# Order of six VectorE instructions in a convolution's input transform, and a GpSimd addition in four pieces instead of two

## The chip, the cores and the metric

The kernel runs on one core of a Trainium2 chip. A core has five engines that work in parallel, each through its own queue in order: TensorE (PE, matrix products; PEld is its weight load), VectorE (DVE), ScalarE (ACT), GpSimd (POOL) and SyncE (SP, which here only issues transfers). They meet at semaphores. The metric is the device time of one execution in microseconds; lower is better.

## The reference

Input x is 32 x 128 x 2048 (batch, channel, length), all in float32. Two residual layers follow each other:

```
x = x + ffn0(cond0(x, c))      # cond0: a 128 x 128 channel mix per batch, a softmax-weighted sum of 8 matrices, plus a bias
                               # ffn0:  out = x W^T + bias, plus 16 low-rank updates scaled by coeffs * scales
x = x + ffn1(cond1(x, c))      # cond1: a grouped convolution over the length, 9 taps, padding 4, 4 groups, plus a context
                               # ffn1:  permuted columns, 16 heads: gelu(t up) down, columns put back
```

## The kernel before, in words

The length is cut into 4 phases of 512 columns (`NPH`, `QW`), and a phase into 4 runs of 128 (`NK`, `NM`). Batches are handled in 8 groups of 4 (`NG`, `GB`).

First, ffn0's weight is multiplied with x by a two-level fast matrix product of seven products each: seven rounds (`ROUNDS`), each over the 8 groups, each of these with seven products in `multiply` (L332). VectorE adds each product to the running sums (L325). Since the weight acts on the length and the mix of cond0 on the channels, this product is made first and the mix is applied to its result.

Then comes a pipeline over the 16 pairs of batches, c = 0 to 15. It begins in the last round, in the gaps that `multiply` leaves after each product (`between`), and goes on between the heads of ffn1 (`ffn_up`, L676, and `ffn_down`, L687). `stage(k, f)` calls a function for every pair with its own step number n = k - (8c - 21), from -2 to 9, so a new pair starts every 8 steps and two pairs overlap. For a pair:

- n = -2 and 1: `mix_loads` brings in one batch each (x, the parts of the product, the mix matrix).
- n = -1 and 2: `mix_bias` adds ffn0's bias `late["fb"]` to x on GpSimd (L427).
- n = 0 and 2: `mix_begin` and `mix_work`: ScalarE presets the banks (L435), TensorE mixes (L444), VectorE adds x (L447), SyncE spreads the result over `xg` (L451).
- n = 4 and 7: `conv_inputs(c, i, 0)` for half i = 0 and 1 of the channels: the six VectorE instructions L513 to L518, "a burst" below. They make from `xg` two difference pairs (each a 128 x 1024 result, an odd part o and an even part e side by side in `vb`) and from these v0 to v3 in `va`.
- n = 5 and 8: `conv_begin` (products of v0, then of v2, L534), and `conv_inputs(c, i, 1)`, which makes the two remaining inputs over `vb`.
- n = 6 and 9: `conv_middle` (products of v1, then of v3), `conv_end` (the two inputs in `vb`), `conv_rows`.

So n = 7 of a pair falls on the same step as n = -1 of the next: the burst of half 1 on VectorE and the bias addition on GpSimd are issued at the same step. In the last round GpSimd has also the sums of x for the next group, `x_combine` (L269 and L296 to L299). In the heads it also issues the indirect transfers of ffn1 (L660, L694).

The order of instructions is the order of the program: the schedule is written out by hand, no planner moves anything. A tile of the slot pool waits for the last readers of what its slot held before.

In the kernel before, both pairs are written to the same half of `vb[c]`, that of index i, one after the other; v1 is made before the second pair overwrites the first.

Of the kernel before, what the change touches and what calls it, by code (L numbers as in the profile page):

```python
# [11 lines left out]
ALU = mybir.AluOpType  # L12
# [12 lines left out]
NPH = 4  # L25
NK = 4
NM = QW // NK
# [24 lines left out]
def adaln_ffn_kernel(  # L52
# [16 lines left out]
    nc = tc.nc  # L69
# [8 lines left out]
    def slot(name, shape=(P, L)):  # L78
        return big.tile(list(shape), FP, name=name, tag="s")
# [314 lines left out]
    late, ins, pms, xgs, x1ts, va, vb, hts, open_ = {}, {}, {}, {}, {}, {}, {}, {}, {}  # L394
# [28 lines left out]

    def mix_bias(b):
        xt = ins[b][1]
        for f in (0, 2):
            nc.gpsimd.tensor_tensor(  # L427
                xt[:, f : f + 2], xt[:, f : f + 2], late["fb"][:, f : f + 2], ALU.add
            )

    def mix_begin(b):

# [63 lines left out]
    def conv_inputs(c, i, part):  # L496

        xg = xgs[c][i].rearrange("p r j n -> p (r j) n")
        d = [xg[:, :, k * NM : (k + 1) * NM] for k in range(NK)]
        tt, stt = nc.vector.tensor_tensor, nc.vector.scalar_tensor_tensor  # L500
        low, high = xg[:, :, 0 : 2 * NM], xg[:, :, 2 * NM : 4 * NM]
        if i == 0 and part == 0:
            vb[c] = slot(f"vb_{c}", (P, 2, 2, 4 * NM))
        if part == 0:
            va[c, i] = slot(f"va_{c}{i}", (P, 4, 4 * NM))
            v = [va[c, i][:, q].rearrange("p (r m) -> p r m", r=4) for q in range(4)]

            oe = vb[c][:, i].rearrange("p q (r m) -> p (q r m)", r=4).rearrange(
                "p (r k m) -> p r k m", r=4, k=2
            )  # L510
            o, e = oe[:, :, 0], oe[:, :, 1]
            both = oe.rearrange("p r k m -> p r (k m)")
            stt(both, low, -4.0, high, ALU.mult, ALU.add)  # L513
            tt(v[0], e, o, ALU.add)  # L514
            tt(v[1], e, o, ALU.subtract)  # L515
            tt(both, high, low, ALU.subtract)  # L516
            stt(v[2], o, 2.0, e, ALU.mult, ALU.add)  # L517
            stt(v[3], o, -2.0, e, ALU.mult, ALU.add)  # L518
        else:
            v0, v5 = (vb[c][:, i, q].rearrange("p (r m) -> p r m", r=4) for q in range(2))  # L520
            stt(v0, d[1], -5.0, d[3], ALU.mult, ALU.add)
            stt(v5, d[2], -1.25, d[0], ALU.mult, ALU.add)
            w0, w5 = v0[:, :, 1:NM], v5[:, :, 0 : NM - 1]
            stt(w0, d[3][:, :, 0 : NM - 1], 4.0, w0, ALU.mult, ALU.add)
            stt(w5, d[0][:, :, 1:NM], 0.25, w5, ALU.mult, ALU.add)
# [83 lines left out]
    def stage_first(c, n):  # L609
        if n in (-2, 1):  # L610
            mix_loads(2 * c + (n == 1))
        if n in (-1, 2):
            mix_bias(2 * c + (n == 2))
# [19 lines left out]
    def third_rest(c, n):  # L633
        if n in (6, 9):
            conv_rows(c, int(n == 9))
        if n == 3:
            residual_rows(c, 0, 0)
            residual_rows(c, 0, 1)
        if n in (4, 5, 7, 8):
            conv_inputs(c, int(n > 5), n in (5, 8))  # L640
        if n in (4, 5):
            residual_rows(c, 1, n - 4)
        if n == 8:
            xgs.pop(c)
# [326 lines left out]
    for k, (g, h) in enumerate(heads):  # L971
# [5 lines left out]
        t = ts.pop(k)  # L977
# [75 lines left out]
```

## Time and profile before

| | us |
|---|---|
| median of 3 runs (lowest to highest) | 2651.13 (2650.91 to 2654.36) |
| the profiled execution, its own time | 2649.93 |
| its span, from the first to the last instruction | 2648.2 |
| bias on GpSimd, L427, 64 instructions of 128 x 1024 | 155.5, mean 2448 ns |
| difference pairs on VectorE, L513 and L516, 32 each | 55.4 and 42.0, mean 1733 and 1313 ns |
| v0, v1 (L514, L515), 32 each | 35.3 and 25.1, mean 1103 and 784 ns |
| v2, v3 (L517, L518), 32 each | 25.0 and 26.2, mean 780 and 818 ns |

The mean granted clock of TensorE was 0.997 of full. In the profile, a line of a view names the engine, the line of the kernel, the operation, what it writes and reads (`va<-vb`), its shape and, in brackets, how long the engine had been idle before and what ended that. A float32 matmul of 128 x 512 runs as two instructions.

### The profile page before, as it was taken

How to read it: one execution, taken by the hardware profiler on the slowest of the kernel's cores; microseconds unless marked ns; L12 is line 12 of the kernel's file. 1: busy time of each engine (PE TensorE's matmuls, PEld its weight loads, DVE VectorE, ACT ScalarE, POOL GpSimd, SP SyncE). 2: the span in 40 equal slices, each digit the busy share in tenths (PEclk: the TensorE clock that was granted, in tenths of full speed). 3: DMA queues.
4: the chain of work that ended last, by engine and by line, in shares of the span. 5: the costliest groups of instructions: out<-in, count | busy, mean ns of one | idle time of the engine just before them, and what ended most of it. 6: DMA issues, size and time to landing. Idle time of an engine off the chain costs nothing.

```text
span 2648.2 us, 20100 instructions
## 1 busy us (share of the span) xinstructions
PE 2620.2 (99%) x6484; PEld 1234.3 (47%) x6484; DVE 1335.3 (50%) x2168; ACT 535.2 (20%) x1103; POOL 1200.2 (45%) x950
## 2 busy tenths in 40 slices
PE   9999999999999999999999999999999999999998
PEld 4444444444444444444444445555455544555543
DVE  5554134343233454433366666666666666666610
ACT  0000000000000000000011144444444444444432
POOL 7321536978756644756332333333433333333222
PEclk9999999999999999999999999999999999999999
DMA  8542458688466577565657788777678777777532
GB/s 317 201 163 103 163 194 325 266 327 351 153 247 254 221 284 288 222 256 201 226 203 240 221 304 283 234 220 232 228 248 255 224 227 227 239 240 237 164 126 88
DMA packets 183609, 609.18 MB, mean 230 GB/s; under 512 B 16848, under 2 KB 88016, under 8 KB 139088
## 3 DMA queue, kind: packets, MB, share of 16 engines
q1 hardware_dynamic: 150080, 474.79, 50.8%
q0 software_dynamic: 32992, 132.14, 14.5%
q8 instruction: 52, 0.85, 0.1%
q10 hardware_dynamic: 432, 0.96, 0.1%
q14 instruction: 53, 0.43, 0.0%
HBM read 372.42 MB, written 201.85 MB: 217 GB/s over the span
## 4 chain that ended last, share of the span: by engine, by line
PE 95%; DVE 2%; DMA 1%; issue 1%; SPq 0%; ACT 0%; POOLq 0%; DVEq 0%; ACTq 0%
PE bank L332 49%; PE bank L676 16%; PE bank L687 16%; PE bank L534 6%; PE bank L444 4%; PE bank L210 2%; PE bank L172 1%; DMA xg<-x 1%; DVE va L514 0%; DVE vb L513 0%; DVE vb L516 0%; DMA ws<-in_ffw 0%; DVE va L515 0%; DVE va L517 0%; DMA bf_sb<-in_BfT 0%
## 5 line engine op out<-in xcount | busy, mean ns | idle before, releaser
L676 PE MATMUL bank<-t,ws 128*128 128x512 f32 x1024 | 460.7, 593 | 1.0 <-DVE u L325 0.5
L687 PE MATMUL bank<-gl,ws 128*128 128x512 f32 x1024 | 460.2, 592 | 0.0
L694 POOL DMA_INDIRECT out<-t,orow x128 | 151.7, 1185 | 562.3 <-DVE t L692 493.8
L325 DVE TENSOR_TENSOR u<-bank,u 128x512 f32<-128x512 f32 x280 | 187.6, 688 | 418.0 <-PE bank L332 411.0
L679 ACT ACTIVATE gl<-bank 128x512 f32<-128x512 f32 x512 | 306.0, 598 | 447.3 <-PE bank L676 445.1
L332 PE MATMUL bank<-P_t,s_P 128*128 128x512 f32 x896 | 393.7, 592 | 0.0
L687 PEld LDWEIGHTS bank<-gl,ws 128*128 128x128 f32 x1024 | 194.8, 190 | 232.7 <-issue 230.8
L676 PEld LDWEIGHTS bank<-t,ws 128*128 128x128 f32 x1024 | 194.6, 190 | 228.0 <-issue 219.2
L332 PE MATMUL bank<-wo_P,s_P 128*128 128x512 f32 x640 | 283.1, 595 | 1.5 <-DVE u L325 1.5
L332 PE MATMUL bank<-wo_P,xt 128*128 128x512 f32 x640 | 281.5, 592 | 0.0
L332 PEld LDWEIGHTS bank<-P_t,s_P 128*128 128x128 f32 x896 | 170.5, 190 | 213.2 <-issue 211.2
L435 ACT ACTIVATE bank<-w,aggb 128x512 f32<-128x512 f32 x128 | 80.8, 684 | 890.2 <-DVE ags L406 872.6
L427 POOL TENSOR_TENSOR x<-x,fb 128x1024 f32<-128x1024 f32 x64 | 155.5, 2448 | 226.1 <-DMA x<-in_x 176.1
L692 DVE TENSOR_TENSOR t<-bank,t 128x512 f32<-128x512 f32 x128 | 87.9, 687 | 318.0 <-PE bank L687 318.0
L269 POOL TENSOR_TENSOR xt<-xt,xt 128x512 f32<-128x512 f32 x128 | 159.6, 1280 | 157.7 <-DMA xt<-in_xT 157.7
L332 PE MATMUL bank<-P_t,xt 128*128 128x512 f32 x448 | 201.5, 593 | 0.0
L325 DVE TENSOR_TENSOR p<-bank,p 128x512 f32<-128x512 f32 x112 | 77.5, 692 | 238.8 <-PE bank L332 238.8
L296 POOL TENSOR_TENSOR s_P<-xt 128x512 f32<-128x512 f32 x56 | 71.8, 1283 | 272.1 <-DMA xt<-in_xT 215.8
L332 PEld LDWEIGHTS bank<-wo_P,s_P 128*128 128x128 f32 x640 | 122.3, 191 | 154.2 <-issue 152.5
L332 PEld LDWEIGHTS bank<-wo_P,xt 128*128 128x128 f32 x640 | 121.7, 190 | 152.1 <-issue 150.1
L406 DVE SCALAR_TENSOR_TENSOR ags<-mix,att_bc,ags 128x128 f32<-128x128 f32 x224 | 155.9, 696 | 4.5
L660 POOL DMA_INDIRECT t<-hx_d,row x128 | 124.8, 975 | 59.9 <-issue 24.7
(144 smaller groups left out, 2649.6 us busy)
## 6 DMA issues: line engine op xcount, KB each, us to landing
xt<-in_xT SPq DMA_DIRECT2D x88, 1024.0 KB, 8.9
u<-u_d SPq DMA_DIRECT2D x40, 1024.0 KB, 11.3
wo_P<-wb_d SPq DMA_DIRECT2D x36, 1024.0 KB, 14.2
u<-c_d SPq DMA_DIRECT2D x64, 512.0 KB, 5.9
x<-in_x SPq DMA_DIRECT2D x32, 1024.0 KB, 8.0
xg<-x SPq DMA_DIRECT2D x256, 128.0 KB, 5.6
hx_d<-x1t SPq DMA_DIRECT2D x32, 1024.0 KB, 5.3
hx_d<-ht SPq DMA_DIRECT2D x32, 1024.0 KB, 7.0
```

The source lines that it names most:

```text
L269: nc.gpsimd.tensor_tensor(out[:, i, j], a[:, i, j], b[:, i, j], op)
L325: nc.vector.tensor_tensor(to, ps, to, ALU.add)
L332: nc.tensor.matmul(ps, lhsT=lhs[k][:, bass.ts(kc, P)], rhs=rhs[k][kc], start=first and kc == 0, stop=last and kc == 3, skip_group_check=True,)
L406: nc.vector.scalar_tensor_tensor(ag, mix[:, k], att, ag, ALU.mult, ALU.add)
L427: nc.gpsimd.tensor_tensor(xt[:, f : f + 2], xt[:, f : f + 2], late["fb"][:, f : f + 2], ALU.add)
L444: nc.tensor.matmul(pm, lhsT=ag, rhs=u[:, f], start=False, stop=True, skip_group_check=True)
L534: nc.tensor.matmul(out, lhsT=w[:, 2 * i + r], rhs=rhs, start=first and r == 0, stop=last and r == 1, skip_group_check=True,)
L660: nc.gpsimd.indirect_dma_start(out=t.rearrange("p k t -> p (k t)"), out_offset=None, in_=hx_d[g].rearrange("l k t -> l (k t)"), in_offset= ...
L676: nc.tensor.matmul(pu, lhsT=w[:, m * P : (m + 1) * P], rhs=t[:, 0], start=True, stop=True)
L679: nc.scalar.activation(gl[m], pu, AF.Gelu)
L687: nc.tensor.matmul(pd, lhsT=w[:, (MC + m) * P : (MC + m + 1) * P], rhs=gl[m], start=(m == 0), stop=(m == MC - 1),)
L694: nc.gpsimd.indirect_dma_start(out=out, out_offset=bass.IndirectOffsetOnAxis(ap=orow[:, g, h : h + 1], axis=0), in_=t[:, 1], in_offset=None,)
```

## The change

The six instructions of a burst are put in another order. The first pair is written to the other half of `vb[c]`, 1 - i, and the second to half i, so that both are there at the same time; v1 is made after v2. The bias is added in four instructions of 128 x 512 in place of two of 128 x 1024. Sizes, tiles, and everything on TensorE, ScalarE and SyncE stay the same. In the changed kernel v0, pair 2, v2, v1 and v3 stand in lines L514 to L518 in this order; the bias is again L427.

```diff
     def mix_bias(b):
         xt = ins[b][1]
-        for f in (0, 2):
-            nc.gpsimd.tensor_tensor(
-                xt[:, f : f + 2], xt[:, f : f + 2], late["fb"][:, f : f + 2], ALU.add
-            )
+        for f in range(NPH):
+            nc.gpsimd.tensor_tensor(xt[:, f], xt[:, f], late["fb"][:, f], ALU.add)
...
-            oe = vb[c][:, i].rearrange("p q (r m) -> p (q r m)", r=4).rearrange(
-                "p (r k m) -> p r k m", r=4, k=2
-            )
-            o, e = oe[:, :, 0], oe[:, :, 1]
-            both = oe.rearrange("p r k m -> p r (k m)")
-            stt(both, low, -4.0, high, ALU.mult, ALU.add)
-            tt(v[0], e, o, ALU.add)
-            tt(v[1], e, o, ALU.subtract)
-            tt(both, high, low, ALU.subtract)
-            stt(v[2], o, 2.0, e, ALU.mult, ALU.add)
-            stt(v[3], o, -2.0, e, ALU.mult, ALU.add)
+            oes = [
+                vb[c][:, h].rearrange("p q (r m) -> p (q r m)", r=4).rearrange(
+                    "p (r k m) -> p r (k m)", r=4, k=2
+                )
+                for h in (1 - i, i)
+            ]
+            (o0, e0), (o1, e1) = ((t[:, :, 0:NM], t[:, :, NM : 2 * NM]) for t in oes)
+            stt(oes[0], low, -4.0, high, ALU.mult, ALU.add)
+            tt(v[0], e0, o0, ALU.add)
+            tt(oes[1], high, low, ALU.subtract)
+            stt(v[2], o1, 2.0, e1, ALU.mult, ALU.add)
+            tt(v[1], e0, o0, ALU.subtract)
+            stt(v[3], o1, -2.0, e1, ALU.mult, ALU.add)
```

## The prediction

> **What bounds the kernel now.** I read the page first, for the share of each engine and the chain that ended last, then the waits of TensorE alone, then the timeline around the longest of them. The profiled execution has a span of 2648.2 us.
>
> ```profile
> PE 2620.2 (99%) x6484; PEld 1234.3 (47%) x6484; DVE 1335.3 (50%) x2168; ACT 535.2 (20%) x1103; POOL 1200.2 (45%) x950
> ...
> PE 95%; DVE 2%; DMA 1%; issue 1%; SPq 0%; ACT 0%; POOLq 0%; DVEq 0%; ACTq 0%
> ```
>
> TensorE is busy for 99% of the span, and the change leaves its instructions and their order as they are. So only what TensorE waits for can be won. The waits of TensorE:
>
> ```profile
> PE bank L534 <- DVE va L517: 7.8, 6, 3.8
> PE bank L210 <- DVE w L213: 4.7, 3, 4.0
> PE bank L332 <- DVE u L325: 1.5, 1, 1.5
> ...
> PE bank L534 <- ACT cq L545: 1.3, 1, 1.3
> ...
> PE bank L676 <- DVE u L325: 0.5, 1, 0.5
> PE bank L676 <- DMA ws<-in_ffw: 0.4, 1, 0.4
> ```
>
> Columns: total us, times, longest. The L210 wait lies in the first 50 us, outside the change. The rest, 7.8 + 1.5 + 1.3 + 0.5 + 0.4 = 11.5 us, lies where convolution and mixing run. Its main part is the second product of conv_begin (L534) waiting for v2 (L517). By the timeline the six waits for L517 end at 1384.58 (3.80 us), 1441.17 (1.41), 1474.29 (0.46), 1525.27 (0.90), 1769.83 (0.56) and 2421.72 (0.67); the one put down to cq ends at 1915.68 (1.29), 0.15 us after that burst's v2 (1914.84 + 0.69), so it is a seventh. The longest, as the timeline has it (start, length, engine, line):
>
> ```profile
> 1372.71 5.63 POOL L427 TENSOR_TENSOR x<-x,fb 128x1024 f32<-128x1024 f32 x2 [27.51 <-DMA x<-in_x]
> ...
> 1373.70 2.44 DVE L513 SCALAR_TENSOR_TENSOR vb<-xg 128x1024 f32<-128x1024 f32 x1
> 1376.18 2.72 DVE L514 TENSOR_TENSOR va<-vb 128x512 f32<-128x512 f32 x1
> 1378.31 1.72 POOL L296 TENSOR_TENSOR s_P<-xt 128x512 f32<-128x512 f32 x1
> 1378.82 1.75 DVE L515 TENSOR_TENSOR va<-vb 128x512 f32<-128x512 f32 x1
> 1379.76 1.03 PE L534 MATMUL bank<-va,tw_l 128*128 128x256 f32 x4
> ...
> 1380.60 2.17 DVE L516 TENSOR_TENSOR vb<-xg 128x1024 f32<-128x1024 f32 x1
> ...
> 1382.81 1.63 DVE L517 SCALAR_TENSOR_TENSOR va<-vb 128x512 f32<-128x512 f32 x1
> ...
> 1384.58 1.35 PE L534 MATMUL bank<-va,tw_l 128*128 128x256 f32 x4 [3.80 <-DVE va L517]
> 1385.73 4.65 PE L444 MATMUL bank<-u,agl 128*128 128x512 f32 x7
> ```
>
> Two things are to be seen. First, VectorE and GpSimd take turns: L514 takes 2.72 us here and 0.69 in a burst with no GpSimd work beside it (the burst at 1520.7), and each DVE instruction ends about when the POOL one before it has ended plus its own time. The burst reaches v2 after 10.7 us; undisturbed ones take 4.5. Second, the wait costs more than its 3.80 us: the chain of waits gives the eight L444 matmuls after it 4.87 us and eight others 3.43, and the four L534 take 1.35 where after a short wait they take 1.10. That is 1.44 + 0.25 = 1.69 us of TensorE at reduced pace.
>
> **The skill.** "SBUF — State Buffer", section "Who interferes with whom": a DVE instruction with two SBUF inputs and a GpSimd one that reads SBUF exclude each other for a whole instruction. The trace agrees: L513 to L518 stretch, while L325 with its PSUM operand takes 0.69 beside a running L427. "TensorE: Matmul & The Clock Gate", "What's actually happening": after about 3.4 us idle the array runs at half rate. The trace agrees after 3.80 us, and shows the same after two waits of 1.41 and 1.47 close together (eight L332 from 1443.77 take 5.14 us for 3.43), which the section doesn't lead one to expect.
>
> **The change, part by part.**
>
> *Order of the six DVE instructions.* Now: difference pair 1, v0, v1, pair 2, v2, v3. Then: pair 1, v0, pair 2, v2, v1, v3. The same six, so v0 and the end of the six stay where they are; v2 comes one instruction earlier: 0.69 us undisturbed, 1.67 with a turn of GpSimd in between (L515's end, 1380.57, less L514's, 1378.90). v1 and v3 are read by conv_middle at the next step, v3 being the later in both orders, so v1's delay costs nothing; v3 is no later, and covers it. For half 1, pair 1 is written over what conv_end of half 0 reads; the VectorE instructions of that conv_end (L586, L589) already stand ahead in the same queue and need those products, so nothing new is waited for. This covers all 32 bursts.
>
> *The bias in four pieces.* 32 inputs x 4 = 128 POOL instructions for 64. A lone 128x512 takes 1.28 us (L269, L296) against 2.35 for a 128x1024 (L427's median): 4 x 1.28 - 2 x 2.35 = 0.4 us more per input, 13 us in all on an engine at 45%, hidden by its idle time. If that cover were gone it would be 13 us, but GpSimd's products, s_P, are read four products of 1.72 us or more later. What counts is the turn-taking: a burst that begins beside L427 now loses to two pieces of 2.35; afterwards each of four DVE instructions lets one short piece past. The price of a piece in turn is the unknown. Below, from this trace: L515 ends 1.67 after L514 and L517 1.67 after L516 (1382.77 to 1384.44), L516 2.20 after L515, each with one 512 piece (L296 to L298) in between; less 0.65 or 1.22 that is about 1.0 us. Above: the whole 1.28. I take 1.0, since it was measured at just such turns; the other end is the first rival. A gain of more than that is excluded by the alternation.
>
> *The seven waits afterwards.* First: piece one from 1372.71 to 1373.99, pair 1 to 1375.21, piece and v0 to 1376.88, piece and pair 2 (2.20) to 1379.08, piece and v2 to 1380.75; plus 0.14 to TensorE 1380.89. TensorE was ready at 1384.58 - 3.80 = 1380.78. So 3.7 of 3.80 go, and the reduced pace with them: 5.4 us.
> At 1474.29: v2 is a turn (1.67) earlier, wait gone, 0.46 + 0.23 for restarting the array (1.10 against 0.87 for four) = 0.7.
> At 1441.17: v2 is 1.3 earlier and the wait goes, but the next product, at 1443.77, waits 1.47 us for an L325 queued on VectorE behind the whole six and the transposes after them (the GpSimd work beside them is x_combine's, unchanged). It now waits 2.8: nothing won.
> At 1525.27: the same in small, L325 takes it back at 1527.78: nothing.
> The other three are of one kind:
>
> ```profile
> 1760.90 5.65 POOL L427 TENSOR_TENSOR x<-x,fb 128x1024 f32<-128x1024 f32 x2 [3.22 <-issue]
> ...
> 1764.37 2.73 DVE L514 TENSOR_TENSOR va<-vb 128x512 f32<-128x512 f32 x1
> ...
> 1769.83 1.10 PE L534 MATMUL bank<-va,tw_l 128*128 128x256 f32 x4 [0.56 <-DVE va L517]
> ```
>
> By the same steps from L513's start (1762.18, a piece just over): 1.22 + 1.67 + 2.20 + 1.67 gives v2 at 1768.94 instead of 1769.69, 0.75 earlier. That is more than 0.56, and than 0.67 at 2421.72; with 0.23 each for the restart 0.8 and 0.9. At 1915.68, 0.8 of 1.29.
> Sum: 5.4 + 0.7 + 0 + 0 + 0.8 + 0.9 + 0.8 = 8.6 us. Span 2648.2 - 8.6 = 2639.6; that execution's own time, 2649.93, becomes 2641.3. The median of the runs is 1.2 above it: 2651.13 - 8.6 = 2642.5.
>
> **The rivals.**
> *The turns cost the full 1.28.* Then v2 of the first burst comes at 1373.99 + 1.22 + 1.97 + 2.50 + 1.97 = 1381.65, the wait is 1.0, and 2.8 + 1.7 = 4.5 us are won; 0.7 at 1474; at 1762 v2 would be at 1769.84, no gain. Together 5.2: 2645.9. For: one lone piece is 1.28. Against: the measured turns.
> *Won, then given back.* TensorE is 5.4 us ahead from 1385 on and meets transfers that don't move with it. For: L427 waits 176.1 us for x in all, so transfers come close to the work. Against: the loads stand on SP's queue behind a store that waits for L325 (505.4 us over 36 times), which moves with TensorE. Only the later 0.7 + 2.5 stays: 2648.
> *Slower.* From 1690 on eleven bursts run beside L427; v2 then has 0.1 to 0.8 us to spare before TensorE asks for it in eight of them, nothing in three. If each of four turns costs 0.45 more than taken, v2 comes 1.0 later than before instead of 0.8 earlier: 1.0 less the spare of each, about 8 us over the eleven, and no gain at 1384: some 2659. It decides from about 0.75 late. Against: the turns in the trace would have to grow by 45%.
> That the change doesn't do what it says is no case: the instruction streams of the two kernels show v2 as fourth of six and four pieces per input.
>
> **How the numbers follow.** Forecast 0.58, full price 0.20, given back 0.12, slower 0.10. A measurement of this kernel can tell some 0.2%, 5.3 us, from no change. Full price lies on that line and is halved: faster 0.68, same 0.22, slower 0.10. The forecast's own range is 2639 to 2646: below, the wait at 1441 falling away as well, if x_combine's pieces come after the burst (2.9 us of waits and 1.7 of reduced pace at most); above, the input landing 0.5 us later. The range for 8 in 10 is 2637 to 2652, which takes in the first two rivals and leaves the slower one out.
>
> **What would show it.** TensorE's wait for v2 (then L516) of at most some 2 us in all, none over 1.1; the L444 after the first burst at 3.43 us for eight; L514 never above 2.0; the wait for L325 near 1443 grown to 2.8; GpSimd busy some 13 us more. The prediction is wrong if v2 still comes 10 us after the first burst's start, if waits for x or s_P appear on TensorE, or if head bursts reach v2 later than 8 us after their start.

## The result, and the profile after

The changed kernel takes 2638.9 us (median; 2637.23 to 2640.06) against 2651.02 for the kernel before: a ratio of 0.9953, 95% interval 0.9944 to 0.9963, so 9.8 to 14.8 us faster where 8.6 was forecast. The profiled execution has a span of 2635.5 us, 12.7 less. The page of the kernel after, engines' shares and the chain that ended last:

```profile
PE 2614.5 (99%) x6484; PEld 1230.3 (47%) x6484; DVE 1336.4 (51%) x2168; ACT 535.3 (20%) x1103; POOL 1230.7 (47%) x1014
...
PE 96%; DVE 2%; DMA 1%; issue 0%; SPq 0%; POOLq 0%; ACT 0%; DVEq 0%; ACTq 0%
```

TensorE is the bound as before, with the same 6484 instructions. GpSimd is busy 30.5 us longer. TensorE's waits in the kernel after (total us, times, longest):

```profile
PE bank L332 <- DVE u L325: 3.1, 1, 3.1
...
PE bank L534 <- DVE va L516: 0.7, 2, 0.5
PE bank L676 <- DMA ws<-in_ffw: 0.4, 1, 0.4
```

The wait for v2, now L516, is 0.7 us where it was 7.8 and the 1.3 put down to cq. The wait for L325 has grown from 1.5 to 3.1. The first burst in the timeline after:

```profile
1371.65 7.36 POOL L427 TENSOR_TENSOR x<-x,fb 128x512 f32<-128x512 f32 x4 [28.86 <-DMA x<-in_x]
1372.11 1.89 DVE L513 SCALAR_TENSOR_TENSOR vb<-xg 128x1024 f32<-128x1024 f32 x1
1374.03 1.64 DVE L514 TENSOR_TENSOR va<-vb 128x512 f32<-128x512 f32 x1
1375.60 2.28 DVE L515 TENSOR_TENSOR vb<-xg 128x1024 f32<-128x1024 f32 x1
1377.91 1.64 DVE L516 SCALAR_TENSOR_TENSOR va<-vb 128x512 f32<-128x512 f32 x1
1378.17 1.03 PE L534 MATMUL bank<-va,tw_l 128*128 128x256 f32 x4
...
1379.70 1.10 PE L534 MATMUL bank<-va,tw_l 128*128 128x256 f32 x4 [0.50 <-DVE va L516]
1380.64 3.60 PE L442 MATMUL bank<-u,agl 128*128 128x512 f32 x8
```

v2 is the fourth of the six and comes 7.4 us after the start instead of 10.7. Each VectorE instruction takes its turn after one short piece: 1.64 for 512 columns, 2.28 for 1024. The matmuls that follow the wait run at full pace (eight in 3.60 us by the timeline, whose last end overlaps the next; before, seven took 4.65). The burst in the heads that answers to the one at 1762 us:

```profile
1751.08 7.36 POOL L427 TENSOR_TENSOR x<-x,fb 128x512 f32<-128x512 f32 x4 [3.73 <-DMA x<-in_x]
...
1757.34 1.64 DVE L516 SCALAR_TENSOR_TENSOR va<-vb 128x512 f32<-128x512 f32 x1
...
1759.13 1.10 PE L534 MATMUL bank<-va,tw_l 128*128 128x256 f32 x4 [0.19 <-DVE va L516]
```

To compare kernels I use one number from each trace: the time that TensorE lost from 1300 us on, which is the distance between the starts of two neighbouring matmuls less the usual 0.43 us (0.21 for 256 columns), summed where it is above 0.04. It holds a wait, the restart after it and a stretch at reduced pace, in which a matmul takes longer than usual. Place by place, before and after:

| place (time before) | before | after | forecast gain | gain |
|---|---|---|---|---|
| first burst, 1384 | 5.7 | 0.7 | 5.4 | 5.0 |
| 1441 and 1444 | 4.8 | 3.4 | 0 | 1.5 |
| 1474 | 0.7 | 0 | 0.7 | 0.7 |
| 1525 and 1528 | 2.0 | 0.4 | 0 | 1.6 |
| heads, from 1600 | 3.3 | 0.9 | 2.5 | 2.4 |
| all, with the ws wait of 0.7 in both | 17.3 | 6.1 | 8.6 | 11.2 |

The other 1.5 us of the span were gone before 1300: the pipeline's very first burst, for half 0 of the first pair and with no bias beside it, begins at 1342.9 instead of 1344.4, before the change can act. It is a difference between two executions: in other profiles that burst begins between 1343.2 and 1347.4.

One profile is one execution, and two later ones show how far such places shift. The kernel before once more (e10) lost 17.9 us from 1300 us on, 6.3 of them at 1441 and 1444 and only 1.3 in the heads; the changed kernel once more (e7) lost 8.4 us, 5.1 of them at the place of 1441 and 1444, 1.1 at that of 1525 and 1528, and 0.7 in the heads.

### The profile page after: what moved, and what is told of

The parts are those of the page before. It is cut to its first block, busy times and chain, and to the rows that moved or that the text cites. A ratio compares the mean times of both kernels' runs of the same rounds, so it can differ in the third digit from the quotient of the medians.

```text
span 2635.5 us, 20243 instructions
## 1 busy us (share of the span) xinstructions
PE 2614.5 (99%) x6484; PEld 1230.3 (47%) x6484; DVE 1336.4 (51%) x2168; ACT 535.3 (20%) x1103; POOL 1230.7 (47%) x1014
## 3 DMA queue, kind: packets, MB, share of 16 engines
q0 software_dynamic: 32992, 132.14, 14.8%
## 4 chain that ended last, share of the span: by engine, by line
PE 96%; DVE 2%; DMA 1%; issue 0%; SPq 0%; POOLq 0%; ACT 0%; DVEq 0%; ACTq 0%
PE bank L332 50%; PE bank L676 16%; PE bank L687 16%; PE bank L534 6%; PE bank L442 4%; PE bank L210 2%; PE bank L172 1%; DMA xg<-x 1%; DMA ws<-in_ffw 0%; DVE vb L515 0%; DMA a_sb<-in_A 0%; DVE vb L513 0%; DVE va L514 0%; PE bank L801 0%; DVE va L516 0%
## 5 line engine op out<-in xcount | busy, mean ns | idle before, releaser
L325 DVE TENSOR_TENSOR u<-bank,u 128x512 f32<-128x512 f32 x280 | 187.6, 688 | 415.4 <-PE bank L332 405.7
L427 POOL TENSOR_TENSOR x<-x,fb 128x512 f32<-128x512 f32 x128 | 178.9, 1427 | 223.9 <-DMA x<-in_x 223.9
L325 DVE TENSOR_TENSOR p<-bank,p 128x512 f32<-128x512 f32 x112 | 77.5, 692 | 235.3 <-PE bank L332 232.1
L660 POOL DMA_INDIRECT t<-hx_d,row x128 | 132.3, 1034 | 57.2 <-issue 26.0
```

What stands on the lines that cost most here:

```text
L325: nc.vector.tensor_tensor(to, ps, to, ALU.add)
L427: nc.gpsimd.tensor_tensor(xt[:, f], xt[:, f], late["fb"][:, f], ALU.add)
L660: nc.gpsimd.indirect_dma_start(out=t.rearrange("p k t -> p (k t)"), out_offset=None, in_=hx_d[g].rearrange("l k t -> l (k t)"), in_offset= ...
```

## The experiments

### One part at a time

The theory is turn-taking at the port that VectorE and GpSimd share: the order saves v2 one instruction and its turn, the cut makes each turn shorter. Rivals: one of the two does it all.

Only the order (e1), the bias left in two pieces (the diff is against the kernel after):

```diff
-        for f in range(NPH):
-            nc.gpsimd.tensor_tensor(xt[:, f], xt[:, f], late["fb"][:, f], ALU.add)
+        for f in (0, 2):
+            nc.gpsimd.tensor_tensor(
+                xt[:, f : f + 2], xt[:, f : f + 2], late["fb"][:, f : f + 2], ALU.add
+            )
```

> Only the new order of the six instructions; the bias stays in two pieces of 1024 columns. Theory (both parts count, through turns at the shared port): in the first burst v2 follows pair 1, v0 and pair 2 behind two long pieces and one of x_combine: about 9.0 us after the burst's start instead of 10.7, the wait there about 2.1 us instead of 3.8, with or without the reduced pace after it (1.7); the wait of 0.46 near 1474 gone; in the heads v2 comes 0.6 earlier, so waits of 0.56, 0.67 and 1.29 become 0, 0.1 and 0.7. Together 5 to 9 us faster than before, some 2642 to 2646, and slower than the full change by 3 to 7. Rival, the order alone does it: 2639, wait at the first burst under 0.6. Rival, the pieces alone do it: within 2 us of before, waits as before.

Measured: 2645.34 us, 0.9981 of before (0.9974 to 0.9988). TensorE's waits in e1 (L536 is conv_begin's product there, L518 v2):

```profile
PE bank L536 <- DVE va L518: 3.4, 5, 1.9
PE bank L332 <- DVE u L325: 3.3, 1, 3.3
PE bank L149 <- DVE warm L146: 1.5, 1, 1.5
PE bank L678 <- DVE u L325: 1.1, 1, 1.1
```

v2 of the first burst comes after 8.9 us and the wait there is 1.94, as worked out (9.0 and 2.1). The wait near 1474 is gone.

Only the cut (e2), in the kernel before:

```diff
-        for f in (0, 2):
-            nc.gpsimd.tensor_tensor(
-                xt[:, f : f + 2], xt[:, f : f + 2], late["fb"][:, f : f + 2], ALU.add
-            )
+        for f in range(NPH):
+            nc.gpsimd.tensor_tensor(xt[:, f], xt[:, f], late["fb"][:, f], ALU.add)
```

> Only the bias in four pieces of 512 columns; the old order (v2 fifth of six). Theory: in the first burst v2 comes behind five VectorE instructions and as many turns: about 8.7 us after its start, the wait about 1.8 us instead of 3.8, with or without the reduced pace (1.7); the wait near 1474 stays at about 0.5 (no bias beside that burst); in the heads v2 comes no more than 0.1 earlier than before, so waits of about 0.5 stay. Together 2 to 7 us faster than before, 2644 to 2649. Rival, the pieces alone do it: 2639 with all waits gone. Rival, the order alone does it: within 2 us of before.

Measured: 2644.45 us, 0.9979 of before (0.9969 to 0.9988). TensorE's waits in e2 (L532 and L515 are conv_begin's product and v2):

```profile
PE bank L532 <- DVE va L515: 4.4, 4, 2.2
...
PE bank L332 <- DVE u L325: 1.5, 1, 1.5
```

v2 of the first burst comes after 9.2 us (8.7 worked out), the wait is 2.22; the waits of 1.41, 1.47 and 0.47 stay as they were. In the heads the expectation missed: one wait of 0.29 is left, not several of 0.5. Over the eleven bursts that run beside the bias there, v2 comes 6.8 us after the start on average before, 6.4 in e2, 6.2 in e1 and 6.0 after. But in e10, the kernel before once more, it is 6.4 as well, so these averages do not show what either part is worth in the heads.

So neither part alone does it. 5.2 us (e1) and 6.0 (e2) make 11.2 together; the full change has 12.1 in its own comparison and 11.3 in e7's.

### No bias at all

e3 is the kernel before with the call of the bias addition left out, so that its output lacks ffn0's bias:

```diff
     def stage_first(c, n):
         if n in (-2, 1):
             mix_loads(2 * c + (n == 1))
-        if n in (-1, 2):
-            mix_bias(2 * c + (n == 2))
```

> The kernel before, old order, with ffn0's bias left out altogether: GpSimd makes no addition to x, so x reaches the residual without that bias. Theory: the waits in the heads are all due to turns with the bias, so every burst there takes its undisturbed 4.5 us to v2 and none waits; the first burst still takes turns with x_combine and reaches v2 after about 7.5 us, wait about 0.6 us; bursts near 1432 and 1466 as before. Some 8 to 10 us faster than before, about 2642. Rival, the length of the burst itself sets the waits (not GpSimd): waits in the heads of 0.5 us and more remain.

Measured: 2637.06 us, 0.9951 of before (0.9936 to 0.9967). All TensorE waits of e3 from 1300 us on:

```profile
PE bank L332 <- DVE u L325: 1.3, 1, 1.3
...
PE bank L534 <- DVE va L517: 0.5, 1, 0.5
...
PE bank L674 <- DMA ws<-in_ffw: 0.2, 1, 0.2
```

With the old order and no bias, every burst of the heads takes 4.5 us to v2 and nothing waits there. GpSimd's addition is what stretches them, not the burst's own length. The gain, 13.4 us, is above the 8 to 10 expected, and the expectation missed two places. The first burst was undisturbed too (4.5, not 7.5): with no bias ahead of it in the queue, x_combine was done at 1370.9, before the burst began at 1372.4. And in the next burst v2 came after 5.5 us, not after 8.4 as before, so that of the two waits and the reduced pace near 1440, 4.8 us before, a wait of 1.25 and its restart were left.

### How finely the bias is cut

The new order, with one addition of 2048 columns per input (e5) and with eight of 256 (e6):

```diff
-        for f in range(NPH):
-            nc.gpsimd.tensor_tensor(xt[:, f], xt[:, f], late["fb"][:, f], ALU.add)
+        nc.gpsimd.tensor_tensor(xt, xt, late["fb"], ALU.add)                    # e5
...
+        for f in range(NPH):                                                    # e6
+            for h in (slice(0, NQ), slice(NQ, QW)):
+                nc.gpsimd.tensor_tensor(xt[:, f, h], xt[:, f, h], late["fb"][:, f, h], ALU.add)
```

> The new order, the bias in one instruction of 128 x 2048 for each input (about 4.5 us from the 1.08 us that each further 512 columns cost). Theory of turns: in the first burst pair 1 waits for the whole piece, then v0, pair 2 and v2 take turns with x_combine: v2 about 10.4 us after the start, wait about 3.5 us; in the heads one long turn only, so v2 comes between 5 and 8.5 us after the start, by how late in the piece the burst begins. Some 4 to 6 us slower than the full change, 2643 to 2645. Rival, only the sum of GpSimd's work beside a burst counts, not its cut: v2 at about 7.5 us and 2639.

> The new order, the bias in eight instructions of 128 x 256 (about 0.7 us each, from the same slope). Theory of turns: each of the four VectorE instructions lets one short piece past, about 0.45 us in turn; v2 of the first burst about 5.5 to 6 us after its start, no wait there; heads at most 6 us. About 1 us faster than the full change, since only 0.5 + 0.2 + 0.1 us of waits for v2 and their restarts are left there: 2637 to 2638.5. Rival, the sum of GpSimd's work counts, or a short piece has a fixed cost near that of a long one: v2 at 7.4 us or later, time 2639 or more.

The first burst in the timeline of e6 (L514 to L517 are pair 1, v0, pair 2, v2):

```profile
1373.29 9.28 POOL L428 TENSOR_TENSOR x<-x,fb 128x256 f32<-128x256 f32 x8 [28.54 <-DMA x<-in_x]
1373.68 1.42 DVE L514 SCALAR_TENSOR_TENSOR vb<-xg 128x1024 f32<-128x1024 f32 x1
1375.13 1.10 DVE L515 TENSOR_TENSOR va<-vb 128x512 f32<-128x512 f32 x1
...
1376.15 1.74 DVE L516 TENSOR_TENSOR vb<-xg 128x1024 f32<-128x1024 f32 x1
1377.93 1.10 DVE L517 SCALAR_TENSOR_TENSOR va<-vb 128x512 f32<-128x512 f32 x1
...
1379.74 1.89 PE L535 MATMUL bank<-va,tw_l 128*128 128x256 f32 x8
```

v2 comes after 5.35 us, and conv_begin's eight matmuls run through without a wait. A turn costs 1.10 - 0.69 = 0.4 us here, against 1.64 - 0.69 = 0.95 with 512 columns. In the eleven head bursts v2 comes after 5.2 to 5.7 us, 4.9 to 7.1 after the change, 4.5 to 8.0 in e5: the finer the cut, the narrower the spread, because it matters less where in a piece the burst begins. GpSimd's bias takes 216.0 us in e6 and 145.4 in e5, so it is not the sum of its work that counts. The time of e6 is 2639.11, above the 2637 to 2638.5 expected and 0.7 less than the full change beside it (2639.77): within their spread. So the shorter turns are shown by the trace, a shorter time than the full change's is not.

e5 takes 2652.06 us, 0.9997 of before (0.9989 to 1.0006), and so is worse than expected. Its first burst:

```profile
1376.15 4.51 POOL L426 TENSOR_TENSOR x<-x,fb 128x2048 f32<-128x2048 f32 x1 [25.53 <-DMA x<-in_x]
1378.83 2.92 DVE L512 SCALAR_TENSOR_TENSOR vb<-xg 128x1024 f32<-128x1024 f32 x1
...
1387.44 1.10 PE L533 MATMUL bank<-va,tw_l 128*128 128x256 f32 x4 [1.52 <-DVE va L515]
```

The burst began 2.7 us into the piece, so v2 took 8.5 us and not 10.4. What the expectation missed lies elsewhere: a wait of 1.98 at 1355 for L325 with a reduced pace behind it, three waits of 0.7 to 0.8 in the heads, and one of 0.9 at 1582 of ffn_down's product for the mix's addition (L444 there, L447 before). With one piece the bias costs all that the new order brings.

### What is left: L325 behind the burst

After the change the longest wait is 3.14 us at 1437.19. The forecast took it to be one for an addition queued behind the whole burst and its transposes. In e4, during the last round, v1, v3 and the transposes of the residual are issued one product later, behind that addition:

```diff
-            tt(v[1], e0, o0, ALU.subtract)
-            stt(v[3], o1, -2.0, e1, ALU.mult, ALU.add)
+            def rest():
+                tt(v[1], e0, o0, ALU.subtract)
+                stt(v[3], o1, -2.0, e1, ALU.mult, ALU.add)
+
+            put_off(rest)
...
-            residual_rows(c, 1, n - 4)
+            put_off(lambda: residual_rows(c, 1, n - 4))
...
         def between(j):
+            catch_up()
```

`put_off` keeps a function for the next `catch_up` in the last round, and calls it at once in the heads.

> The full change, and in the last round v1, v3 and the transposes of the residual are issued one product later, behind VectorE's next addition. Theory: what is left of TensorE's waits, 3.1 us at 1437, is for an addition (L325) queued behind the whole burst and its transposes; with v1, v3 and four transposes out of its way (about 2.7 us and one turn of 1.0 or two) the wait falls to 0 to 1 us. Some 1.5 to 3 us faster than the full change, 2636 to 2637.5. Rival, that wait is set by TensorE's own order or by a transfer: it stays at 3 us and the time at 2639. Rival, the put-off work delays the addition after it by as much: a new wait for L325 one product later, time within 1 us of the full change.

> The full change as it is, beside the next three on one chip. Theory: 2639 (2637 to 2641), v2 of the first burst 7.4 us after its start, TensorE's wait there about 0.5 us, one wait of some 3 us for L325 near 1437 in the last round, with or without a stretch at reduced pace after it; the wait at the burst near 1510 to 1525 depends on when the last xg transfer lands. Rival, the extra 1.5 us won near 1525 belong to the change and not to that transfer: the wait there is again under 0.3 us whatever the transfer takes.

> The same kernel as e4, beside the full change on one chip. Theory: 3 to 4 us faster than the full change, 2635 to 2636, with no wait of TensorE for L325 in the last round. Rival, the difference between e4 and the full change was one of chips: within 1.5 us of it.

e4 takes 2635.11 us, 0.9937 of before (0.9924 to 0.9951). e7 is the full change and e8 is e4 once more, side by side: 2639.77 us (2637.37 to 2642.19) and 2635.51 (2632.35 to 2636.20), 0.9952 (0.9938 to 0.9965) and 0.9935 (0.9922 to 0.9949) of before. The spreads don't overlap; it is 4.3 us. No wait for L325 is left from 1300 us on in e4 and e8, and no new one came. Lost time there is 1.9 and 2.1 us, 8.4 in e7. The 4.3 us are more than the wait near 1437 alone, which is 3.1 us: in e7's profile 5.1 us went with its reduced pace and 1.7 near 1525, and at both places e4 and e8 lose nothing.

Both remedies, eight pieces and the put-off work (e9):

> Both remedies at once: the put-off work of e4 and the bias in eight pieces of 256 columns. Theory: e4's remaining waits for v2 (0.1 to 0.8 us with their restarts) go, some 1 us faster than e4: 2634 to 2635, and TensorE waits for nothing over 0.2 us from 1300 us on. Rival, GpSimd's longer total (some 20 us more than with two pieces) makes its own products or gathers late: new waits for s_P or t, time 2636 or more.

2633.86 us, 0.9931 of before (0.9918 to 0.9945). All waits of TensorE in e9's whole span:

```profile
PE bank L210 <- DVE w L213: 4.7, 3, 4.0
PE bank L172 <- DMA bf_sb<-in_BfT: 1.7, 1, 1.7
PE bank L149 <- DVE warm L146: 1.5, 1, 1.5
PE bank L210 <- DVE ctxb L797: 0.3, 1, 0.3
```

All four lie in the first 250 us; from 1300 us on no time is lost at all. From there to the end TensorE waits for nothing, so nothing more is to be won in this part by moving work on the other engines. e9 is 18 us faster than the kernel before beside it (2652.0), and its slowest execution, 2635.82, is below the fastest of the full change (2637.23). It is 1.3 us below e4 and 1.7 below e8, which were not measured together with it, and the spreads overlap, so that step by itself is not shown.

### The kernel before once more

> The kernel before, for a second profile. Theory: v2 of the first burst again some 10 us after its start with a wait of 3 to 4 us there, the pair of waits of 1.4 and 1.5 us near 1440 again, two to four waits of 0.3 to 1.3 us in the heads, at other bursts than before; a stretch at reduced pace after the waits near 1384 and 1444 not necessarily both. Rival, the first profile was an odd one: no wait over 2 us there.

One execution, 2651.16 us. v2 of the first burst comes again after 10.7 us, and the wait is 3.79; then come 1.41, 1.47 and 0.46, and 1.35 at the burst near 1525; in the heads other bursts wait than before, and less (0.34 and 0.24). Lost time from 1300 us on is 17.9.

### The reduced pace

TensorE in e7 and in the profile of the full change, the same wait at the same place:

```profile
1440.02 5.37 PE L332 MATMUL bank<-wo_P,s_P 128*128 128x512 f32 x8 [3.15 <-DVE u L325]
```

```profile
1437.19 3.67 PE L332 MATMUL bank<-wo_P,s_P 128*128 128x512 f32 x8 [3.14 <-DVE u L325]
```

After 3.15 us of idling the eight matmuls take 5.37 us in one execution, after 3.14 they take 3.67 in another of the same kernel. Likewise 1.41 and 1.47 close together were followed by 5.14 for eight in the kernel before, and in e10 and e2 by:

```profile
1445.01 6.59 PE L332 MATMUL bank<-wo_P,s_P 128*128 128x512 f32 x8 [1.47 <-DVE u L325]
```

```profile
1440.04 3.67 PE L332 MATMUL bank<-wo_P,s_P 128*128 128x512 f32 x8 [1.47 <-DVE u L325]
```

The reduced pace came after the wait of 1.98 in e5 and not after those of 1.94 (e1) and 2.22 (e2); it came after the longest wait of the kernel before in both profiles (3.80, and 3.79 in e10). So between about 2 and 3.3 us of idling it may or may not come; it cost 1.4 to 1.8 us most times and 2.9 in e10. The Trainium skill, "TensorE: Matmul & The Clock Gate", "What's actually happening", says of its idle window that it is "free-running". That fits a pace that changes from one execution to the next; no run here shows the window itself, and the 1.98 us of e5 are shorter than the 3.4 us that the prediction takes from that section, so on the length of idling the measurement decides.

### Part of the 1.6 us near 1525

There the burst waits for the last transfers into `xg`, and TensorE then for L325. From the end of the mix's last addition to the start of that burst 17.0 us pass before, 15.5 after; the wait for L325 just before the heads follows it with the new order: 15.4 us and 0 (e6), 15.5 and 0.13 (after), 16.2 and 0.78 (e7), 16.75 and 1.12 (e5), 17.1 and 1.12 after 0.24 for v2 (e1). So the place goes with that transfer, as e7's expectation had it, and almost half of the gain there was gone in e7. In the four profiles with bias pieces of 1024 or 2048 columns the stretch is 16.75 to 17.5, in the seven with shorter pieces (e2, e4 and e6 to e9 among them) 15.4 to 16.2, and in e3, without the bias, 14.9. They don't overlap. From the first of the mix's four additions to the burst the DMA engines moved 5.2 to 5.4 MB in all twelve profiles, at 262 to 270 GB/s with the longer pieces and 273 to 286 with the shorter ones or none; so it is the rate that differs more than the amount. Why the bias should touch it, when it is done 0.8 to 3.1 us before the mix's additions, was not found. It stays open.

## Why the prediction was right, and where it was off

The direction and the range for 8 in 10 held, and the mechanism held where it could be followed, at the first burst and at 1474. The median, 2638.9, lies just under the forecast's own range of 2639 to 2646; what the prediction named for a time so low, the wait at 1441 falling away, did not happen. By its steps:

- *What can be won.* Right: only TensorE's waits. The forecast counted the waits as 11.5 us; with restarts and reduced pace they are 17.3, and e9, with none of them and 18 us faster, shows that they can all be had.
- *The order.* Right: v2 sooner by one instruction or turn, v0 and the end unchanged (the first burst's six end after 10.8 us in e2 and after, 12.4 and 12.2 before and in e1, so that is the cut's doing); no wait on v1 or v3, none for `vb`. Alone 5.2 us.
- *The cut.* Right: a turn costs about 1.0 (0.95 measured at v0 and v2), not the whole 1.28, so the first rival falls. Alone 6.0 us. Wrong was GpSimd's 13 us: its additions are also stretched by their own waiting, so the bias went from 155.5 to 178.9 us, and the indirect transfers at L660 took 7.5 us longer; it is 30.5 in all. TensorE waited for none of it.
- *The first burst.* 5.0 us for 5.4. The burst began 0.5 us after the bias instead of 1.0, so the wait was 0.50 instead of 0.1. In e7 it was 0.69.
- *1441.* The wait moved to L325 as worked out (2.8; 3.14 measured) and nothing was won by it. The 1.5 us of the table are the reduced pace that didn't come in this execution and did in e7. The step that failed took it as fixed to the wait.
- *1525.* Nothing was forecast; 1.6 us came, 0.9 in e7, with a shorter time for the transfers into `xg`. The term left out is that time, taken over unchanged from the profile before.
- *Heads.* 2.4 for 2.5 us is luck. Which bursts wait, and how long, changes from one execution to the next, since it depends on where in a piece a burst begins; the forecast took the waits of one execution for those of the kernel. In e10 only 1.3 us were lost there and not 3.3, and against that the gain is 0.4 us, or 0.7 with e7.
- *Given back* and *slower.* Neither came: TensorE met no new transfer, and turns didn't grow.

From 1300 us on the profile after gained 11.2 us, 2.6 more than forecast: 1.6 at 1525 and 1.5 at 1441, less 0.4 at the first burst and 0.1 in the heads. It is of the fastest of six executions. e7's profile, of the slowest of its five, lost 8.9 us less than the profile before, close to the forecast. The medians lie between these two executions; how the 3.5 us between forecast and median are shared out among the places is not shown.

## What to carry to other kernels

On a kernel bound by one engine, list that engine's waits, and for each follow the queue of the engine that releases it: what stands ahead of the one instruction that is waited for, and what of it can go behind. Where two engines take turns, as VectorE and GpSimd do here, the cut of the one's work sets the delay of the other per instruction; halving the pieces of the engine with time to spare is worth about as much here as a better order on the other, even though it makes the first one busier. Take a second profile of the kernel before, too: which of the small waits it has is partly chance, and a forecast made wait by wait from one execution can be right for the wrong reason. And look where a wait goes: once the work in the way of L325 was put off, another 4 us were won.

## What had not been expected of the hardware

A reduced pace of TensorE came after some waits of 2.0 to 3.3 us and not after others, in one case of the same length at the same place of the same kernel; it cost 1.4 to 1.8 us, and once 2.9. And a GpSimd addition in turns with VectorE costs VectorE less than its own length: 0.95 us for one of 1.28, 0.4 for one of 256 columns, which takes 0.72 (the median in e6). So the two do not shut each other out for quite the whole instruction, as the prediction took it.
